# Two residual additions moved to TensorE with an identity and written out by ScalarE, in a convolution-attention and selective-scan kernel

## The chip, the cores and the metric

The kernel runs on one core of one Trainium2 chip. The time is the device time of one execution in microseconds (us). A core has five engines with a queue each: TensorE (PE; its weight loads are shown apart as PEld), VectorE (DVE), ScalarE (ACT), GpSimd (POOL) and SyncE (SP), which here issues nearly all DMA transfers. PSUM is the memory that TensorE writes; POOL's instructions in this kernel never touch it.

## The reference, cut to what is computed

Eight images of 256 channels and 48 x 48 = 2304 positions pass through two residual layers:

```
x = x + attention(groupnorm(x))            # layer 0
x = x + mamba2(mamba1(groupnorm(x)))       # layer 1, two scan blocks

def attention(x):                          # per image, tokens: 2304 x 256
    feat, pos = split(tokens @ W.T + bias)          # 2304 x 256 each
    pos = pos / max(norm(pos), 1e-12)
    sim = pos @ pos.T                               # 2304 x 2304
    topksim, topkid = top_k(sim, 16)
    return softmax(topksim) weighted sum of feat[topkid]

def mamba(x):                              # 2304 positions, 512 inner channels, 16 states
    x = layernorm(x) * w + b
    xi, z = split(x @ in_w.T)
    xc = silu(causal_conv4(xi) + cb)
    dt_r, B, C = split(xc @ xp_w.T);  dt = softplus(dt_r @ dtp_w.T + dtp_b)
    h[t] = h[t-1] * exp(dt[t] * A) + dt[t] * B[t] * xc[t]
    y = sum over states of h * C + D * xc
    return (y * silu(z)) @ out_w.T
```

The two additions that the change concerns are `x + attention(...)` and the last `x + ...` after the second scan block.

## The kernel before

**Outline.** Layer 0 of image 0 runs alone at the start (`layer0(0, ..., True)`, about the first 470 us). After that the scans of image b run together with layer 0 of image b + 1, instruction by instruction, in an order written out by hand. The last image's scans have no layer 0 beside them.

**The scan's units and half-steps.** Positions are cut into 6 chunks of 384. A *unit* is one chunk of one scan block, so that an image has 12 units, numbered 0 to 11 here in their order (c, d) = (0,0), (1,0), (2,0), (0,1), (3,0), (1,1), (4,0), (2,1), (5,0), (3,1), (4,1), (5,1); d is the scan block. A unit has 16 steps of two *half-steps*, 32 half-steps in all, called h0 to h31 below. There are 8 x 12 x 32 = 3072 half-steps. In each one DVE runs one scan instruction (`run_scan`, L843; 770 elements on 128 partitions).

**What surrounds a scan.** ACT writes its decays into one of two PSUM areas with two exponentials (`decay`, L828), one half-step ahead; POOL makes the scan's input for two half-steps at once (`make_bx`, L804), two steps ahead. The product of the states with C is made either by POOL (L871, in `pool_part`, for one or both half-steps of a step at once) or by DVE (L845, right behind the scan). Which, is set by `SHARE`: one letter for each half-step, G for POOL (GpSimd) and V for DVE. It has three patterns, for units 1 to 9 of images 0 to 6 (called stage 0 here), for units 0, 10 and 11 of these (stage 1), and for the last image (stage 2). In a V half-step the scan writes the PSUM area, and ACT takes the last state from there (`carry`, L859); otherwise `carry_pool` (L881) takes it from SBUF. TensorE then sums the states (`sum_states`, L886 and L889) into a PSUM tile `y`, which DVE multiplies into z (`gate`, L895). The tables `between` and `behind` place all other work of a unit on half-steps relative to its first; `between` runs ahead of the scan of its half-step and `behind` after it.

**The first block's way out.** `out_proj` (L907, at 38, so in h6 of the next unit) makes the two outputs `pw` of 128 channels in PSUM, and `leave` (at 39 and 40, h7 and h8 of the next unit) brings each out. For d = 0 ACT copies it to SBUF (L920) and SP stores it. For d = 1 DVE adds it to the residual `res`, loaded in `load_out` (L924), and SP stores it to the output.

**Layer 0 beside the scans.** `layer0` is a generator that is advanced once at the end of each half-step (`ahead.go`). Its attention works on 18 blocks of 128 rows per image. The table `within` gives each piece of a block a part, block t's part p being executed in half-step 38 + 16 t + p of the image: `similar` makes the 5 pieces of a row of similarities (TensorE, tile `psim`), `keep_similar` copies them out (ACT, L408), `top` finds the 16 greatest (DVE, 4 instructions of 2304 elements), `average` scales the weighted sum (ACT, tile `o`) and loads the block of x (tile `xr`), `turn_back` transposes `o` into the PSUM tile `pr` (L482), and `finish` (part 24, so h14 or h30) adds `pr`, the bias and `xr` on DVE (L491), takes the statistics (L495) and has SP store the sum to `x1`. When all blocks are done, `group_stats` spreads over 8 half-steps; `load_v` of the next image's first unit, 42 half-steps ahead of it, calls `ahead.finish`, which runs whatever of the generator is left.

**PSUM slots.** All these PSUM tiles (`pe`, `pw`, `y`, `psim`, `pr`, `pt` and so on) share one tag "mm" of 3 slots when layer 0 runs beside scans (5 when it runs alone). A tile can be written only when an earlier tile's last reader is done.

Of the kernel before, what the change touches and what calls it, by code (L numbers as in the profile page):

```python
# [10 lines left out]
AF = mybir.ActivationFunctionType  # L11
ALU = mybir.AluOpType
# [3 lines left out]
P = 128  # L16
# [9 lines left out]
def tile_conv_preact(  # L26
# [18 lines left out]
    nc = tc.nc  # L45
    B, C, N = x.shape
    DEPTH, DI, NS = A_log.shape
# [3 lines left out]
    CB = C // P  # L51
    DB = DI // P
# [5 lines left out]
    G = 32  # L58
# [4 lines left out]
    PARTS = Q // HQ  # L63
# [4 lines left out]
    BLOCK = 16  # L68
# [1 line left out]
    PHASE = 6  # L70


    SHARE = ("GGVGGGVVGGGGGGVG", "GGGVGVVGVVVGVGVG", "VGVGVGVVGGVVGGVG")
    assert N % T == 0 and N % P == 0 and T % P == 0 and NS % (J * HQ) == 0

    const = ctx.enter_context(tc.tile_pool(name="const", bufs=1))
# [10 lines left out]
    ident = const.tile([P, P], F32, tag="ident", name="ident")  # L87
# [32 lines left out]
    b_feat = const.tile([P, CB], F32, tag="b_feat", name="b_feat")  # L120
# [109 lines left out]
    def layer0(b, left, pool, ps0, alone):  # L230
        def mm0(w, name):
            return ps0.tile([P, 512], F32, tag="mm", name=name, bufs=5 if alone else 3)[:, :w]
# [159 lines left out]
        blocks = [{} for _ in range(NB)]  # L392
# [85 lines left out]
        def turn_back(t):  # L478
            row = blocks[t]
            row["pr"] = mm0(C, f"pr_{b}_{t}")  # L480
            for cb in range(CB):
                nc.tensor.transpose(  # L482
                    row["pr"][:, cb * P : (cb + 1) * P], row["o"][:, cb * P : (cb + 1) * P], ident
                )

        def finish(t):
            row = blocks[t]
            xr = row["xr"]

            for cb in range(CB):  # L490
                nc.vector.scalar_tensor_tensor(  # L491
                    xr[:, cb, :], row["pr"][:, cb * P : (cb + 1) * P], b_feat[:, cb : cb + 1],
                    xr[:, cb, :], ALU.add, ALU.add,
                )
                nc.vector.bn_stats(st1[:, cb, t, :], xr[:, cb, :])  # L495
            nc.sync.dma_start(x1[:, t * P : (t + 1) * P].rearrange("(k p) t -> p k t", p=P), xr)
            row.clear()


        within = [  # L500
            (21, weights, 3), (4, top, 3), (14, turn, 0), (15, weights, 0), (6, others, 3),
            (-5, similar, 4), (-8, keep_similar, 0), (-5, keep_similar, 2), (24, turn_back), (18, weigh, 1),
            (17, weigh, 0), (1, top, 1), (-9, similar, 0), (-8, similar, 1), (-7, similar, 2),
            (22, average), (-6, similar, 3), (-7, keep_similar, 1), (-3, keep_similar, 3), (0, top, 0),
            (-3, keep_similar, 4), (15, turn, 1), (10, others, 4), (5, others, 0), (3, top, 2),
            (6, add_top), (11, invert), (5, others, 2), (17, turn, 2), (20, turn, 3),
            (15, weights, 1), (18, turn, 4), (18, weights, 2), (21, weigh, 3), (7, others, 1),
            (19, weigh, 2), (20, weights, 4), (21, weigh, 4), (24, finish),
        ]
        begin = min(part for part, *_ in within)  # L510
        parts = {}
# [13 lines left out]
    with tc.tile_pool(name="first", bufs=1) as pool0, tc.tile_pool(  # L525
        name="first_ps", bufs=1, space=PSUM
    ) as ps0:
        for _ in layer0(0, lefts[0], pool0, ps0, True):
            pass
# [28 lines left out]
    def mm(w, name):  # L558
        return ps.tile([P, 512], F32, tag="mm", name=name, bufs=3)[:, :w]
# [232 lines left out]
    def on_pool(unit, i, p):  # L792

        stage = 2 if unit["b"] + 1 == B else 0 if TOPK[0] <= unit["at"] < TOPK[1] else 1
        return SHARE[stage][(i * PARTS + p) % BLOCK] == "G"

    def make_bx(n):

# [34 lines left out]
    def run_scan(m):  # L833
        n, p = divmod(m, PARTS)
        if not 0 <= n < NSTEP:
            return
        unit, i, k = at(n)
        qs = slice(p * HQ, (p + 1) * HQ)
        bx = unit["bx"][i][:, qs]
        g = bx.rearrange("p q t -> p (q t)")  # L840
        da = decays(m)
        h = g if on_pool(unit, i, p) else da
        nc.vector.tensor_tensor_scan(h, da, g, 0.0, ALU.mult, ALU.add)  # L843
        if h is da:
            nc.vector.tensor_tensor(  # L845
                bx[:, :, 0:T], da.rearrange("p (q t) -> p q t", q=HQ)[:, :, 1:],
                unit["BC"][1][:, qs], ALU.mult,
            )

    def carry(m):  # L850

        n, p = divmod(m, PARTS)
        if not 0 <= n < NSTEP:
            return
        unit, i, k = at(n)
        if not on_pool(unit, i, p):
            h = decays(m).rearrange("p (q t) -> p q t", q=HQ)
            if unit["c"] + 1 < NCH:
                nc.scalar.copy(h_st[:, unit["d"], i, p * HQ : (p + 1) * HQ], h[:, :, T])  # L859

    def pool_part(n):

        if not 0 <= n < NSTEP:
            return
        unit, i, k = at(n)
        lo = [p for p in range(PARTS) if on_pool(unit, i, p)]
        if not lo:
            return
        qs = slice(lo[0] * HQ, (lo[-1] + 1) * HQ)
        g = unit["bx"][i][:, qs]  # L870
        nc.gpsimd.tensor_tensor(g[:, :, 0:T], g[:, :, 1:], unit["BC"][1][:, qs], ALU.mult)  # L871
# [31 lines left out]

    def out_proj(unit, cb):
        pw = unit["pw"][cb] = mm(T, f"pw_{unit['u']}_{cb}")
        for k in range(DB):
            nc.tensor.matmul(  # L907
                pw, unit["ow"][:, k, cb * P : (cb + 1) * P], unit["z"][k],
                start=(k == 0), stop=(k == DB - 1),
            )  # L910

    def leave(unit, cb):

        b, c, rows = unit["b"], unit["c"], slice(cb * P, (cb + 1) * P)
        if unit["d"] + 1 < DEPTH:
            v1 = unit["left"].setdefault("v1", {})
            if c not in v1:
                v1[c] = hbm.tile([C, T], F32, tag="v1", name=f"v1_{b}_{c}", bufs=2 * BEHIND)
            vo = keep.tile([P, T], F32, tag="dtx", name=f"vo_{unit['u']}_{cb}")
            nc.scalar.copy(vo, unit["pw"][cb])  # L920
            nc.sync.dma_start(v1[c][rows, :], vo)
        else:
            res = unit["res"]
            nc.vector.tensor_add(res[:, cb, :], res[:, cb, :], unit["pw"][cb])  # L924
            nc.sync.dma_start(out[b, rows, c * T : (c + 1) * T], res[:, cb, :])


# [1 line left out]
    between = [  # L929
        (-35, center), (7, in_proj, 5), (24, sum_states, 2), (-33, variance), (-21, in_proj, 0),  # L930
        (-15, taps, 1), (38, out_proj, 0), (-15, taps, 2), (-14, taps, 3), (-34, square),
        (39, leave, 0), (23, load_rep, "dt", 14), (5, load_rep, "dt", 5), (-4, load_bc, 1), (38, out_proj, 1),
        (17, load_d, 2), (-17, tap, 1), (18, load_rep, "dtx", 13), (-8, times_x, 1), (19, gate, 1),
        (-22, normal), (1, load_rep, "dt", 3), (0, load_rep, "dtx", 4), (15, load_rep, "dt", 10), (6, load_rep, "dtx", 7),
# [12 lines left out]
        (-37, affine), (1, times_x, 2), (7, copy_z, 0), (8, load_rep, "dtx", 8), (-17, tap, 2),  # L947
        (-10, softplus), (-16, in_proj, 3), (3, load_rep, "dt", 4), (-29, load_in, 2), (6, in_proj, 7),
        (35, gate, 3), (-2, load_rep, "dtx", 3), (8, copy_z, 1), (40, leave, 1), (-3, times_x, 3),
        (22, load_rep, "dtx", 15), (-16, load_in, 4), (29, load_d, 3), (-37, mean), (-19, taps, 0),  # L950
        (-19, in_proj, 1), (-10, load_bc, 0), (33, sum_states, 3), (-30, root_end), (-9, times_x, 0),
# [8 lines left out]
    class Ahead:  # L960
# [4 lines left out]
        def turn(self, image):  # L965
            self.image, self.begun, self.started = image + 1, None, False
            self.run = iter(())
            if self.image < B:
                self.run = layer0(self.image, lefts[self.image], keep, ps, False)
# [21 lines left out]
    for m in range(first, PARTS * NSTEP - HOOKS + last + 1):  # L991
        n, p = divmod(m, PARTS)
# [57 lines left out]
```

## Time and profile before

| what | value |
|---|---|
| median of 3 runs | 9905.45 us (9903.67 to 9908.92) |
| the profiled execution: its own time | 9898.83 us |
| its span, first to last instruction | 9897.1 us, mean granted TensorE clock 0.889 |
| first scan / last scan starts at | 517.7 us / 9882.3 us |
| the median unit of stage 0 with d = 1 (5, 7, 9) | about 97 us |
| units 4, 6, 8 of stage 0 | about 99 us |
| units of the last image | about 90 us |
| transfers | 1271 MB, 128 GB/s |

The profile's busy times count no register, branch, semaphore or DMA-issuing instruction. A row "L843 DVE ... bx<-da,bx x2040 | 3521.8, 1746 | 190.5 <-ACT da L828 151.4" says that line 843's instruction on DVE, which writes bx from da and bx, ran 2040 times, 3521.8 us in all and 1746 ns each, and that DVE stood idle for 190.5 us just before such instructions, 151.4 us of it until ACT's line 828 was done. In the waits, "A <- B: us, times, longest" says how long A's engine stood idle until B was done. In the timeline the columns are start, duration, engine, line, operation and how many were merged; the brackets give the idle time just ahead. Consecutive instructions of DVE and ACT overlap in the records by some 0.08 us, so that starts are the better measure of what an instruction costs.

### The profile page before, as it was taken

How to read it: one execution, taken by the hardware profiler on the slowest of the kernel's cores; microseconds unless marked ns; L12 is line 12 of the kernel's file. 1: busy time of each engine (PE TensorE's matmuls, PEld its weight loads, DVE VectorE, ACT ScalarE, POOL GpSimd, SP SyncE). 2: the span in 40 equal slices, each digit the busy share in tenths (PEclk: the TensorE clock that was granted, in tenths of full speed). 3: DMA queues.
4: the chain of work that ended last, by engine and by line, in shares of the span. 5: the costliest groups of instructions: out<-in, count | busy, mean ns of one | idle time of the engine just before them, and what ended most of it. 6: DMA issues, size and time to landing. Idle time of an engine off the chain costs nothing. (4 is left out here: it accounts for less than half of the span.)

```text
span 9897.1 us, 133780 instructions
## 1 busy us (share of the span) xinstructions
PE 8000.3 (81%) x36736; PEld 4388.5 (44%) x36736; DVE 8956.8 (90%) x7993; ACT 7322.2 (74%) x15966; POOL 8943.3 (90%) x3927
## 2 busy tenths in 40 slices
PE   8878887788878888788877888778887788866665
PEld 6644544444534454445444445344544444522222
DVE  4589998999989999899998999899998999988998
ACT  4477777778777877777877787777787778766766
POOL 0099999999989999899998999999998999999999
PEclk9989998899989998899988999889998899977777
DMA  1144445444444444444454444444445444444544
GB/s 32 37 133 126 134 130 152 124 132 129 136 142 131 129 134 137 140 126 133 130 148 128 130 128 134 144 132 125 135 128 152 121 133 127 138 136 129 145 138 122
DMA packets 1243503, 1271.37 MB, mean 128 GB/s; under 512 B 266592, under 2 KB 1215840, under 8 KB 1242752
## 3 DMA queue, kind: packets, MB, share of 16 engines
q1 hardware_dynamic: 1230496, 1262.45, 44.7%
q8 instruction: 293, 4.80, 0.2%
q14 instruction: 458, 3.75, 0.1%
q10 hardware_dynamic: 12256, 0.36, 0.1%
HBM read 1048.94 MB, written 212.86 MB: 127 GB/s over the span
## 5 line engine op out<-in xcount | busy, mean ns | idle before, releaser
L804 POOL TENSOR_TENSOR bx<-BC,dtxr 128x1536 f32<-128x1536 f32 x1536 | 5298.4, 3453 | 115.6 <-PE y L889 59.8
L828 ACT ACTIVATE da<-dtr,A_sb 128x385 f32<-128x385 f32 x6144 | 3591.0, 585 | 871.6 <-DVE bx L843 558.0
L843 DVE TENSOR_TENSOR_SCAN bx<-da,bx 128x770 f32<-128x770 f32 x2040 | 3521.8, 1746 | 190.5 <-ACT da L828 151.4
L871 POOL TENSOR_TENSOR bx<-bx,BC 128x1536 f32<-128x1536 f32 (+1 forms) x1320 | 3303.6, 2503 | 217.5 <-DVE bx L843 205.4
L843 DVE TENSOR_TENSOR_SCAN da<-da,bx 128x770 f32<-128x770 f32 x1032 | 1808.8, 1753 | 193.4 <-ACT da L828 149.0
L602 PE MATMUL pe<-vn,inw 128*128 128x384 f32 (+1 forms) x3072 | 1258.9, 543 | 394.1 <-DVE xr L924 87.0
L399 PE MATMUL psim<-pos 128*128 128x512 f32 (+1 forms) x2880 | 1370.8, 608 | 183.5 <-ACT sim L408 74.7
L465 PE MATMUL po<-feat,aT 128*128 128x256 f32 x5184 | 1364.0, 412 | 13.8 <-ACT aT L454 7.6
L889 PE MATMUL y<-bx,sel 128*32 128x384 f32 x12288 | 1221.2, 533 | 44.2 <-POOL bx L871 37.9
L465 PEld LDWEIGHTS po<-feat,aT 128*128 128x128 f32 x5184 | 1029.8, 205 | 361.9 <-issue 113.9
L845 DVE TENSOR_TENSOR bx<-da,BC 128x768 f32<-128x768 f32 x1032 | 988.8, 958 | 35.5
L602 PEld LDWEIGHTS pe<-vn,inw 128*128 128x128 f32 x3072 | 590.1, 206 | 902.6 <-issue 191.2
L399 PEld LDWEIGHTS psim<-pos 128*128 128x128 f32 x2880 | 552.8, 206 | 818.8 <-issue 470.8
L889 PEld LDWEIGHTS y<-bx,sel 128*32 128x32 f32 x12288 | 394.1, 118 | 856.6 <-issue 725.0
L702 DVE SCALAR_TENSOR_TENSOR xc<-pe,cw,xc 128x384 f32<-128x384 f32 x1152 | 695.7, 611 | 42.8 <-ACT xc L694 15.7
L732 PE MATMUL pd<-dbl,dtp_sb 16*128 16x384 f32 x768 | 424.3, 668 | 342.0 <-ACT dt L741 209.0
L859 ACT COPY h_st<-da 128x2 f32<-128x2 f32 x832 | 131.7, 158 | 686.4 <-DVE bx L845 680.0
L454 ACT ACTIVATE aT<-pt 128x512 f32<-128x512 f32 (+1 forms) x720 | 388.1, 548 | 245.9 <-PE pt L446 239.8
L445 PE MATMUL pt<-ident,sim 128*128 128x128 f32 x2592 | 539.6, 291 | 33.7 <-DVE v L666 17.6
L907 PE MATMUL pw<-z,ow 128*128 128x384 f32 x1536 | 531.5, 499 | 15.0 <-DVE v L666 7.0
L437 ACT ACTIVATE rest<-left,three 128x512 bf16<-128x512 f32 (+1 forms) x720 | 467.0, 670 | 59.7 <-DVE left L422 59.7
L446 PE MATMUL pt<-minus,rest 128*128 128x128 bf16 x2592 | 491.6, 225 | 3.2 <-ACT rest L437 3.2
(146 smaller groups left out, 9766.8 us busy)
## 6 DMA issues: line engine op xcount, KB each, us to landing
dtxr<-dtx_d SPq DMA_DIRECT2D x6144, 48.0 KB, 1.8
dtr<-dt_d SPq DMA_DIRECT2D x6144, 48.0 KB, 1.8
BC<-bc_d SPq DMA_DIRECT2D x768, 192.0 KB, 3.7
inw<-in_in_wT_dram SPq DMA_DIRECT2D x768, 128.0 KB, 2.2
dtx_d<-dtx SPq DMA_DIRECT2D x384, 192.0 KB, 2.0
dt_d<-dt SPq DMA_DIRECT2D x384, 192.0 KB, 2.2
ow<-in_out_wT_dram SPq DMA_DIRECT2D x96, 512.0 KB, 4.0
dmat<-diag SPq DMA_DIRECT2D x384, 64.0 KB, 2.3
```

The lines of the kernel that those rows point to most:

```text
L399: nc.tensor.matmul(pm, pos[:, k, t * P : (t + 1) * P], pos[:, k, c0 : c0 + w], start=(k == 0), stop=(k == CB - 1),)
L445: nc.tensor.transpose(pt[:, q], row["sim"][:, r], ident)
L465: nc.tensor.matmul(row["po"], aT[:, m % PT, :], feat[:, m, :], start=(m == 0), stop=(m == NB - 1))
L602: nc.tensor.matmul(pe, w[:, k], unit["vn"][:, k, lo:], start=(k == 0), stop=(k == CB - 1))
L702: nc.vector.scalar_tensor_tensor(unit["xc"][e], unit["pe"][e][:, k : k + T], cw[:, unit["d"], e, k : k + 1], unit["xc"][e], ALU.mult, ALU.add,
L804: nc.gpsimd.tensor_tensor(bx[:, :, 1:], unit["BC"][0], unit["dtxr"][i].unsqueeze(1).to_broadcast([P, Q, T]), ALU.mult,)
L828: nc.scalar.activation(da[:, s * (1 + T) : (s + 1) * (1 + T)], unit["dtr"][i], AF.Exp, scale=A_sb[:, unit["d"], i, p * HQ + s : p * HQ + s ...
L843: nc.vector.tensor_tensor_scan(h, da, g, 0.0, ALU.mult, ALU.add)
L845: nc.vector.tensor_tensor(bx[:, :, 0:T], da.rearrange("p (q t) -> p q t", q=HQ)[:, :, 1:], unit["BC"][1][:, qs], ALU.mult,)
L871: nc.gpsimd.tensor_tensor(g[:, :, 0:T], g[:, :, 1:], unit["BC"][1][:, qs], ALU.mult)
L889: nc.tensor.matmul(y[j * G : (j + 1) * G, :], sel, unit["bx"][k * J + j][:, q, 0:T], start=False, stop=True, skip_group_check=True,)
L907: nc.tensor.matmul(pw, unit["ow"][:, k, cb * P : (cb + 1) * P], unit["z"][k], start=(k == 0), stop=(k == DB - 1),)
```

## The change

`finish` is split. In `turn_back` TensorE now also adds the block of x to `pr`, by a matmul with the identity, for each of the two channel blocks. `finish`, moved from part 24 to 25, lets ACT write `pr` plus bias to SBUF. The new `measure` at part 26 takes the statistics on DVE and has SP store the block. For the second scan block TensorE adds `res` to `pw` by one more matmul with the identity, and ACT copies the sum out in place of DVE's addition. `SHARE` gives one half-step in 32 more to DVE in stage 0 (h27) and two more in stage 2 (h12 and h28).

```diff
-    SHARE = ("GGVGGGVVGGGGGGVG", "GGGVGVVGVVVGVGVG", "VGVGVGVVGGVVGGVG")
+    SHARE = ("GGVGGGVVGGGGGGVGGGVGGGVVGGGVGGVG", "GGGVGVVGVVVGVGVG", "VGVGVGVVGGVVVGVG")
 # turn_back
                 nc.tensor.transpose(
                     row["pr"][:, cb * P : (cb + 1) * P], row["o"][:, cb * P : (cb + 1) * P], ident
                 )
+                nc.tensor.matmul(
+                    row["pr"][:, cb * P : (cb + 1) * P], ident, row["xr"][:, cb, :],
+                    start=False, stop=True, skip_group_check=True,
+                )
 # finish
             for cb in range(CB):
-                nc.vector.scalar_tensor_tensor(
-                    xr[:, cb, :], row["pr"][:, cb * P : (cb + 1) * P], b_feat[:, cb : cb + 1],
-                    xr[:, cb, :], ALU.add, ALU.add,
-                )
+                nc.scalar.activation(
+                    xr[:, cb, :], row["pr"][:, cb * P : (cb + 1) * P], AF.Identity,
+                    bias=b_feat[:, cb : cb + 1],
+                )
+
+        def measure(t):
+            row = blocks[t]
+            xr = row["xr"]
+            for cb in range(CB):
                 nc.vector.bn_stats(st1[:, cb, t, :], xr[:, cb, :])
             nc.sync.dma_start(x1[:, t * P : (t + 1) * P].rearrange("(k p) t -> p k t", p=P), xr)
 # within
-            (19, weigh, 2), (20, weights, 4), (21, weigh, 4), (24, finish),
+            (19, weigh, 2), (20, weights, 4), (21, weigh, 4), (25, finish), (26, measure),
 # on_pool
-        return SHARE[stage][(i * PARTS + p) % BLOCK] == "G"
+        share = SHARE[stage]
+        return share[(i * PARTS + p) % len(share)] == "G"
 # out_proj
+        alone = unit["d"] + 1 < DEPTH
         for k in range(DB):
             nc.tensor.matmul(
                 pw, unit["ow"][:, k, cb * P : (cb + 1) * P], unit["z"][k],
-                start=(k == 0), stop=(k == DB - 1),
+                start=(k == 0), stop=(k == DB - 1 and alone),
             )
+        if not alone:
+            nc.tensor.matmul(pw, ident, unit["res"][:, cb, :], start=False, stop=True)
 # leave, second scan block
-            nc.vector.tensor_add(res[:, cb, :], res[:, cb, :], unit["pw"][cb])
+            nc.scalar.copy(res[:, cb, :], unit["pw"][cb])
```

## The prediction

> **What bounds the kernel now.** I read the page first, then the busy time unit by unit, then the waits, then the order of time around the two additions.
>
> ```profile
> PE 8000.3 (81%) x36736; PEld 4388.5 (44%) x36736; DVE 8956.8 (90%) x7993; ACT 7322.2 (74%) x15966; POOL 8943.3 (90%) x3927
> ```
>
> DVE and POOL are level, so the page cannot say which one sets the pace. The busy time per unit (units 4 to 7 of image 4; columns: stretch, length, then PE, PEld, DVE, ACT, POOL busy):
>
> ```profile
> 5663.10:5762.30 99.20, 86.89 (x411) 48.91 (x410) 95.29 (x87) 78.21 (x174) 96.36 (x35) 0.93 0.46 131
> 5762.30:5860.80 98.50, 86.93 (x411) 48.69 (x410) 94.46 (x85) 78.00 (x174) 96.36 (x35) 0.93 0.46 130
> 5860.80:5960.00 99.20, 86.91 (x411) 48.98 (x410) 95.30 (x87) 78.20 (x174) 96.36 (x35) 0.93 0.47 133
> 5960.00:6056.70 96.70, 85.76 (x411) 48.19 (x410) 94.35 (x85) 77.56 (x173) 96.33 (x35) 0.94 0.46 130
> ```
>
> POOL has 96.3 us of work in every unit, yet units last 96.7 to 99.2. The waits of units 4 to 9 say who waits for whom:
>
> ```profile
> DVE z L895 <- PE y L889: 9.0, 6, 2.4
> DVE bx L843 <- ACT da L828: 7.0, 11, 1.1
> POOL bx L871 <- DVE bx L843: 8.6, 7, 1.7
> ```
>
> DVE waits for PE and ACT and never for POOL; POOL waits for DVE. So the path is DVE with ACT and PE in its gaps, and POOL follows with some 1 us per unit to spare. In the last image it is the same with more room (its units 2 to 10):
>
> ```profile
> DVE da L843 <- ACT da L828: 31.7, 14, 3.2
> DVE bx L843 <- ACT da L828: 28.5, 15, 3.1
> DVE da L843 <- POOL bx L804: 1.1, 2, 0.6
> ```
>
> There a unit lasts about 90 us, DVE works 80.5 of it and POOL 84.1. The exception is c = 0: in unit 3 POOL clears the first column of the scan's input behind its other work, and DVE waits 5.4 us for that (L816). Layer 0 of image 0 alone is TensorE's: 59.34 us busy of 60 between 300 and 360.
>
> [...] behind an ACT instruction that waited 1.64 us (L694 below) everything on ACT stood. [...] The trace has 468 ns for 256 elements out of PSUM (L472)[...].
>
> **Part 1: `leave` of d = 1.** Removed: L924 on DVE, 96 x 537 ns, 0.46 from start to start. It does more harm than that. In unit 6 the third `pe` needs the slot of `pw`, DVE frees it late behind its top-16 work, and everything behind slides:
>
> ```profile
> 5886.65 2.27 PE L602 MATMUL pe<-vn,inw 128*128 128x384 f32 x4 [1.82 <-DVE xr L924]
> ...
> 5897.32 0.56 DVE L895 TENSOR_TENSOR z<-y,z 128x384 f32<-128x384 f32 x1 [2.44 <-PE y L889]
> ```
>
> In unit 7, where ACT empties `pw` (L920, 468 ns), neither wait is there. The two kinds differ by 1.8 us (units 4, 6, 8 against 5, 7, 9, all images), so units 4, 6, 8 should become like 5, 7, 9. Added on ACT: a copy of 468 ns per tile, beside 2.9 us in which ACT waits for DVE at h7; with that cover gone, 0.9 us a unit. Added on PE: one fp32 matmul of 384 columns per tile, two instructions 0.32 us apart, 1.3 us of PE for a unit; unit 7 has about 1.0 us to spare before z is held, so I count 0.1 against. 21 units x -1.7 = **-36 us**. In units 10, 11 and 0, DVE waits at h10 for PE anyway; -0.9 there is lost, and in unit 10, where PE runs without a gap from `pw` to `y`, the 1.3 us lies on the path: 14 units x 0.7 = +10.
>
> **Part 2: `finish`.** Removed on DVE: L491, 288 x 339 ns. With L495 (292 ns) a block costs DVE 1.17 us; the two statistics alone cost 0.5, so 0.68 goes. Added: two ACT instructions, 0.6 us a block, and four short matmuls, 0.45 us. ACT has the room on average (78 of 97 us), but not at that place. Around h14 of unit 6:
>
> ```profile
> 5906.77 0.44 PE L482 MATMUL pr<-ident,o 128*128 128x128 f32 x2 [0.46 <-ACT sim L408]
> 5908.23 1.98 PE L399 MATMUL psim<-pos 128*128 128x512 f32 x4 [1.02 <-DVE xr L491]
> 5910.89 1.98 PE L399 MATMUL psim<-pos 128*128 128x512 f32 x4 [0.68 <-ACT sim L408]
> ```
>
> ```profile
> 5908.79 1.23 ACT L694 ACTIVATE xc<-pe,cbias,cw 128x384 f32<-128x384 f32 x2
> 5910.25 0.58 ACT L408 COPY sim<-psim 128x512 f32<-128x512 f32 x1 [0.24 <-PE psim L399]
> ...
> 5915.31 0.67 ACT L694 ACTIVATE xc<-pe,cbias,cw 128x384 f32<-128x384 f32 x1 [1.64 <-PE pe L602]
> ```
>
> Two slots hold `pe` here, and the one left goes psim, pr, psim, psim. The next psim starts when `finish` has read `pr`, at 5908.2. On ACT, one half-step on, `finish` stands behind two exponentials and two taps (L694), and ends at about 5910.4. Then psim 2.0, its copy 0.65, psim 2.0, pe 1.5: the last tap starts at about 5916.5 instead of 5915.3, while DVE, 0.68 lighter, wants it sooner. The copy (L408) and the decays behind it wait on ACT meanwhile. The silu and decay burst that DVE waits for at h20 (0.5 us today) starts no earlier. For h14: DVE gains nothing, 0 to +0.6. For h30: `pr` has its own slot, but the copy behind `finish` is 0.3 late, two psim and `y` follow, and the gate at h3 has no room: 0 to +0.3. If the slots left room, it would be -0.68. I take +0.1 x 126 blocks = **+13 us**, with ends of -86 and +57. The identity matmul also waits for `xr`: PE reaches `pr` in half of the blocks within 3 us of the issue of that load, which takes 2.3 to land. PE waits about 1 us there, covered by a gap of 1.5 us ahead of L649; if that is gone, +1 us x 63. SP's store moves two half-steps on and then waits for ACT, no more for DVE (622 us in SP's waits, L496): the transfers behind it can only be earlier, and DVE and ACT hardly wait for them (45.7 us in all): 0. `group_stats` comes two half-steps later, and `ahead.finish` now flushes its last three pieces at once, PE to ACT to POOL in one half-step: 0 to 4 us x 7, I take +5.
>
> **Part 3: `SHARE`.** A V adds L845, 958 ns, 0.9 from start to start (a bare G half-step lasts 1.7 us, a bare V one 2.6), and a 0.16 us copy on ACT. At h27, h12 and h28 DVE has no idle time, so it is paid in full: stage 0, 63 units x 0.9 = **+57**; last image, 24 x 0.9 = **+22**. POOL gets a half product for a whole (1685 for 3184 ns): -1.5 us each, 94 + 36 us. As POOL holds nobody up, that is worth nothing, but for unit 3, where POOL comes to its clearing some 3 us earlier: 7 x -3 = -21, and -3 in the last image.
>
> **Part 4: image 0 alone.** PE is full there: 18 blocks x 0.45 = **+8**. DVE and ACT have room: 0.
>
> **The sum.** 8 + 57 - 36 + 13 - 21 + 10 + 5 + 22 - 3 = +55 us on the profiled execution's 9898.8 (span 9897.1 and 1.7 around it), which lies 0.07% under the median of 9905.45. On the median: 9960 us. What 0.2%, about what a measurement tells from no change, means here is 20 us.
>
> **Rivals.** (A) *The freed DVE time comes through.* ACT has about 2.3 us idle between h27 and h33, PE about 10 a unit; if the slot chain gives room, part 2 is -86 instead of +13: 55 - 99 = -44, 9861 us. For it: unit 1 has no block to finish at h14, and h14 is 1.1 us shorter there with nothing paid back by h20. Against it: unit 1 has no `pr` in the slot either. It decides once more than about half of the 0.68 us comes through. (B) *POOL is the real bound.* It is busy 99% of the shorter units. Then 94 + 36 us less POOL work counts: about -130, 9775 us. Against it: DVE never waits for POOL outside c = 0. (C) *Balance*: half of (A), within 20 us of no change. (D) *PE and ACT tighter than I think*: part 2 at +57, the xr wait uncovered in part, units 0 and 10 at +1.3: +120, 10025 us.
>
> **Numbers.** Slower, as forecast or as (D): 0.52; (C) 0.16; (A) 0.25; (B) 0.07. The range takes in (A) and (D): 9840 to 10030; the forecast's own is 9925 to 10030.
>
> **What would show it.** Right: units 5, 7, 9 about 1 us longer, h27 up by 0.9; units 4, 6, 8 close to them, the wait of `pe` on L924 gone; psim waiting on ACT longer than the 1.0 us it waited on L491; POOL's idle time up by 2 us a unit; the last image up by about 20 us. Wrong: DVE's idle time in units 5, 7, 9 unchanged with DVE's busy time down, or DVE waiting for POOL in the kernel before at places that the records don't show.

## The result and the profile after

The changed kernel takes 10003.24 us (median of 4 runs, 10000.49 to 10011.81), the kernel before 9907.00 us in the same series: a ratio of 1.0099, with a 95% interval of 1.0081 to 1.0116. It is slower by 96 us; 9960 had been forecast, 9840 to 10030 as the range, so the result lies inside it and toward its upper end. The profiled execution has a span of 9998.7 us at a mean granted clock of 0.881.

In the changed kernel `psim` (L399) and the copy of sim (L408) keep their lines. ScalarE's `finish` is L495, the statistics are L504, the identity matmul of `xr` is L485; L828 has become L838 (decay), L843 L853 (scan), L694 L703 (tap), L702 L711 (taps), L889 L899 (y), L895 L905 (gate), L816 L826 (the clearing for c = 0).

The page's busy line:

```profile
PE 8157.6 (82%) x37504; PEld 4525.2 (45%) x37504; DVE 8916.9 (89%) x7696; ACT 7432.4 (74%) x16426; POOL 8823.2 (88%) x3927
```

DVE has 40 us less to do than before, POOL 120 us less; ACT has 110 and PE 157 us more. The two busiest engines are lighter and the kernel is longer, so idle time has been added to the path. Busy time unit by unit (units 4 to 7 of image 4; columns as in the view of before):

```profile
5719.10:5818.50 99.40, 89.45 (x422) 50.76 (x422) 94.47 (x82) 79.94 (x182) 95.05 (x35) 0.91 0.47 132
5818.50:5918.90 100.40, 89.39 (x416) 50.69 (x417) 94.30 (x81) 78.85 (x180) 94.92 (x35) 0.90 0.45 126
5918.90:6018.40 99.50, 88.14 (x426) 50.28 (x425) 94.31 (x82) 80.14 (x183) 95.03 (x35) 0.93 0.47 133
6018.40:6117.40 99.00, 87.16 (x414) 49.63 (x414) 94.23 (x82) 78.50 (x179) 94.89 (x35) 0.92 0.45 127
```

Units 4 and 6 stand where they stood, 5 and 7 are 1.9 and 2.3 us longer, and the difference between the two kinds is gone. (On average over images 0 to 6, units 5, 7 and 9 are 2.8, 2.0 and 1.3 us longer; about 1 had been expected.) POOL now has 4.1 to 5.5 us to spare in each. The waits of units 4 to 9:

```profile
PE psim L399 <- ACT xr L495: 21.3, 11, 3.2
ACT sim L408 <- PE psim L399: 32.7, 15, 3.9
DVE bx L853 <- ACT da L838: 18.0, 21, 1.4
DVE xc L711 <- ACT xc L703: 4.8, 6, 1.4
DVE z L905 <- PE y L899: 3.0, 5, 0.7
```

DVE's wait for `y` has shrunk from 9.0 to 3.0 us (that was the slot which L924 used to hold), its wait for ACT's decays has grown from 7.0 to 18.0, and above them stands a chain that is new in this size: `psim` waits up to 3.2 us for `finish` on ACT, and ACT waits up to 3.9 us for `psim`. In the last image DVE waits for the decays as before:

```profile
DVE da L853 <- ACT da L838: 32.7, 23, 2.3
DVE bx L853 <- ACT da L838: 18.0, 6, 3.1
```

**Where a block loses.** The timeline around h14 to h17 of unit 6 in image 4, the place that the prediction worked through:

```profile
5965.16 1.23 ACT L703 ACTIVATE xc<-pe,cbias,cw 128x384 f32<-128x384 f32 x2
...
5966.28 0.62 ACT L495 ACTIVATE xr<-pr,b_feat 128x128 f32<-128x128 f32 x2
...
5966.95 6.34 PE L399 MATMUL psim<-pos 128*128 128x512 f32 x8 [3.15 <-ACT xr L495]
...
5970.77 0.59 ACT L408 COPY sim<-psim 128x512 f32<-128x512 f32 x1 [3.87 <-PE psim L399]
5971.25 1.21 ACT L838 ACTIVATE da<-dtr,A_sb 128x385 f32<-128x385 f32 x2
...
5972.49 1.76 DVE L853 TENSOR_TENSOR_SCAN bx<-da,bx 128x770 f32<-128x770 f32 x1 [1.44 <-ACT da L838]
...
5974.63 0.67 ACT L703 ACTIVATE xc<-pe,cbias,cw 128x384 f32<-128x384 f32 x1 [0.44 <-PE pe L611]
```

h14 starts at 5961.0 here. `finish` stands behind two taps, and `psim` starts 5.95 us into h14, against 3.6 us before. The four matmuls that its copy needs then take 3.8 us (5966.95 to 5970.7) where they took 1.98. So the copy starts 9.8 us into h14 instead of 5.65, and the decay stands behind it in ACT's queue: DVE waits 1.44 us for it ahead of the scan of h17. The last tap comes 13.6 us in, not 10.7, and DVE's taps wait for that too. Added up over images 0 to 6, DVE waits 49 us for the decays ahead of h17 and 46 us for the last tap behind it; in the kernel before these two waits are 0.2 us together.

### The profile page after: what moved, and what is told of

It reads as the page before. It is cut to its first block, busy times and chain, and to the rows that moved or that the text cites. A ratio compares the mean times of both kernels' runs of the same rounds, so it can differ in the third digit from the quotient of the medians.

```text
span 9998.7 us, 135654 instructions
## 1 busy us (share of the span) xinstructions
PE 8157.6 (82%) x37504; PEld 4525.2 (45%) x37504; DVE 8916.9 (89%) x7696; ACT 7432.4 (74%) x16426; POOL 8823.2 (88%) x3927
## 3 DMA queue, kind: packets, MB, share of 16 engines
q14 instruction: 461, 3.78, 0.1%
## 5 line engine op out<-in xcount | busy, mean ns | idle before, releaser
L838 ACT ACTIVATE da<-dtr,A_sb 128x385 f32<-128x385 f32 x6144 | 3592.0, 585 | 714.2 <-DVE bx L853 365.0
L853 DVE TENSOR_TENSOR_SCAN bx<-da,bx 128x770 f32<-128x770 f32 x1953 | 3382.7, 1749 | 262.9 <-ACT da L838 228.3
L881 POOL TENSOR_TENSOR bx<-bx,BC 128x1536 f32<-128x1536 f32 (+1 forms) x1320 | 3177.8, 2407 | 293.8 <-DVE bx L853 233.8
L853 DVE TENSOR_TENSOR_SCAN da<-da,bx 128x770 f32<-128x770 f32 x1119 | 1962.1, 1753 | 238.4 <-ACT da L838 191.1
L399 PE MATMUL psim<-pos 128*128 128x512 f32 (+1 forms) x2880 | 1433.5, 635 | 248.8 <-ACT xr L495 203.0
L899 PE MATMUL y<-bx,sel 128*32 128x384 f32 x12288 | 1194.6, 527 | 25.8 <-DVE bx L855 19.4
L855 DVE TENSOR_TENSOR bx<-da,BC 128x768 f32<-128x768 f32 x1119 | 1072.2, 958 | 38.5
L399 PEld LDWEIGHTS psim<-pos 128*128 128x128 f32 x2880 | 589.2, 216 | 886.7 <-issue 533.0
L711 DVE SCALAR_TENSOR_TENSOR xc<-pe,cw,xc 128x384 f32<-128x384 f32 x1152 | 697.2, 612 | 87.5 <-ACT xc L703 60.5
L899 PEld LDWEIGHTS y<-bx,sel 128*32 128x32 f32 x12288 | 386.9, 117 | 821.7 <-issue 742.9
L408 ACT COPY sim<-psim 128x512 f32<-128x512 f32 (+1 forms) x720 | 379.9, 536 | 342.4 <-PE psim L399 342.1
L454 ACT ACTIVATE aT<-pt 128x512 f32<-128x512 f32 (+1 forms) x720 | 388.2, 549 | 253.8 <-PE pt L446 249.0
```

What stands on the lines that cost most here:

```text
L399: nc.tensor.matmul(pm, pos[:, k, t * P : (t + 1) * P], pos[:, k, c0 : c0 + w], start=(k == 0), stop=(k == CB - 1),)
L711: nc.vector.scalar_tensor_tensor(unit["xc"][e], unit["pe"][e][:, k : k + T], cw[:, unit["d"], e, k : k + 1], unit["xc"][e], ALU.mult, ALU.add,
L838: nc.scalar.activation(da[:, s * (1 + T) : (s + 1) * (1 + T)], unit["dtr"][i], AF.Exp, scale=A_sb[:, unit["d"], i, p * HQ + s : p * HQ + s ...
L855: nc.vector.tensor_tensor(bx[:, :, 0:T], da.rearrange("p (q t) -> p q t", q=HQ)[:, :, 1:], unit["BC"][1][:, qs], ALU.mult,)
L899: nc.tensor.matmul(y[j * G : (j + 1) * G, :], sel, unit["bx"][k * J + j][:, q, 0:T], start=False, stop=True, skip_group_check=True,)
```

## The experiments

The next table adds up where each kernel's half-steps differ from those of the kernel before, from the starts of DVE's scans in the profiled executions (us; images 0 to 6, all units; the stretch h21 to h24 changes by at most 1.6 and is left out). The last image is counted from its first scan to its last. The last column is the difference of the medians, each against the kernel before in its own series of runs.

| kernel | ahead of the first scan | h4-12 (leave) | h13-20 (finish at h14) | h25-28 (V at h27) | h29-h3 (finish at h30) | last image | medians |
|---|---|---|---|---|---|---|---|
| changed | +11.1 | -18.7 | +77.1 | +63.9 | -48.1 | +17.5 | +96 |
| both additions, old SHARE | +10.3 | -27.0 | +92.1 | +0.3 | -31.6 | +1.6 | +44 |
| new SHARE alone | +1.6 | +12.1 | +7.7 | +64.2 | -22.8 | +16.7 | +73 |
| leave alone | -0.8 | -25.6 | +9.2 | -0.2 | +8.3 | -1.9 | -15 |
| finish alone | +10.8 | +4.4 | +95.3 | -0.2 | -28.8 | -1.9 | +76 |
| early load (below) | -6.1 | -24.3 | -5.3 | 0.0 | -37.8 | -4.2 | -81 |
| clearings on ScalarE (below) | -5.7 | -39.5 | -26.7 | 0.0 | -68.2 | +4.2 | -149 |

A stretch that an edit doesn't touch moves by 9 to 12 us (h13-20 with leave alone, h4-12 with the new SHARE alone), so smaller entries say nothing.

**1. SHARE put back.**

```diff
-    SHARE = ("GGVGGGVVGGGGGGVGGGVGGGVVGGGVGGVG", "GGGVGVVGVVVGVGVG", "VGVGVGVVGGVVVGVG")
+    SHARE = ("GGVGGGVVGGGGGGVG", "GGGVGVVGVVVGVGVG", "VGVGVGVVGGVVGGVG")
```

> The change with the old SHARE put back: leave and finish stay on TensorE and ScalarE, VectorE and GpSimd divide the scan products as in the kernel before. Theory (the path is VectorE's; every half-step turned from G to V is paid at about 0.9 us, and GpSimd's relief is worth only some 10 us): 75 us below the changed kernel, so about 9930 us, still some 25 us above the kernel before. Rival, GpSimd sets the pace: its 130 us of work come back and nothing else, so 10040 us or more. Rival, the losses come from ScalarE and TensorE alone (SHARE costs nothing because VectorE had the freed time to spare): about 10000 us, as the changed kernel.

Measured: 9949.47 us, ratio to the kernel before 1.0050 (1.0033 to 1.0066). SHARE made 52 of the 96 us (96 less 44). GpSimd is not the bound: with its work back the kernel is faster, not slower. The two additions cost 44 us, more than the 25 expected.

**2. The new SHARE alone**, in the kernel before.

> The kernel before with the new SHARE alone; both additions stay on VectorE. Theory (VectorE's path): 63 + 24 more products on VectorE at 0.9 us, less some 10 us for GpSimd's earlier clearing in unit 3: about +70 us, 9975 us. Rival, GpSimd sets the pace: about -100 us, 9800 us. Rival, the new SHARE costs something only because ScalarE and TensorE were made late by the other two parts: within 20 us of the kernel before.

Measured: 9978.26 us, ratio 1.0072 (1.0057 to 1.0087). Its page:

```profile
PE 8007.3 (80%) x36736; PEld 4381.2 (44%) x36736; DVE 9042.8 (91%) x8080; ACT 7357.1 (74%) x16042; POOL 8823.7 (88%) x3927
```

POOL works 120 us less than before, DVE 86 more, and the kernel is 73 us longer: DVE's time is paid, POOL's relief is not repaid. h27 is 1.0 us longer in every one of the 63 units. Units 2 and 3 get 1.0 and 2.0 us shorter in h29 to h3, because POOL comes to the clearing (L816) sooner: -21 us.

**3. Leave of d = 1 alone** (identity matmul into `pw`, ACT's copy).

```diff
-            nc.vector.tensor_add(res[:, cb, :], res[:, cb, :], unit["pw"][cb])
+            nc.scalar.copy(res[:, cb, :], unit["pw"][cb])
```

> The kernel before with the second scan block's addition alone on TensorE and ScalarE (leave of d = 1). Theory: units 4, 6 and 8 are 1.8 us shorter in images 0 to 6, the others as before, units 0, 10 and 11 a little longer: -25 us, 9882 us. Rival (TensorE is the bound here: the identity matmul is added to it and gives back what VectorE gains): within 20 us of the kernel before or above. Rival (all 96 freed additions come through at 0.46 us): -44 us or more on top of the 36, 9825 us.

Measured: 9890.39 us, ratio 0.9987 (0.9980 to 0.9994). Units 4, 6 and 8 are 1.8, 1.9 and 1.8 us shorter in h4 to h12. Units 10 and 11 lose 1.3 and 1.9, unit 0 gains 1.5. In unit 10 of image 4 (h8 to h10) PE runs from `pw` to `y` without a gap, and DVE waits for the decays first and for `y` after that:

```profile
DVE z L895 <- PE y L889: 4.0, 1, 4.0
DVE da L843 <- ACT da L828: 2.5, 1, 2.5
```

The wait for `y` is 4.0 us in the kernel before as well; the wait for the decays was 0.3 there. ACT's copy of `pt` (L454) waits 1.92 us for PE, and the decays stand behind it.

**4. Finish alone** (identity matmul of `xr`, `finish` on ACT at part 25, `measure` at 26).

> The kernel before with the attention's addition alone on TensorE and ScalarE (identity matmul of xr, finish on ScalarE, statistics one half-step later). Theory (the slot of pr is freed late behind ScalarE's queue, so copy of sim, pe and tap are late and VectorE waits at h17, which eats the 0.68 us taken off VectorE): +11 us before the first scan and +0.3 to +0.7 us a block after it, about +45 us, 9952 us. Rival (the freed VectorE time comes through): 126 blocks x -0.68 us + 11 us = -75 us, 9830 us. Rival (loss and gain cancel): +11 us, the first image's part alone, 9917 us.

Measured: 9981.47 us, ratio 1.0077 (1.0062 to 1.0092). It is the dearest part, and it loses at h14 (+95 us, 1.5 a block) while it gains at h30 (-29 us). Taken alone the three parts come to 134 us, together they cost 96: with finish in, leave is worth -32, and the new SHARE costs 52 rather than 73. A part of that can be placed: with finish alone, DVE's wait for POOL's clearing at h31 of unit 2 grows from 5.5 to 13.6 us (seven images), and in the changed kernel, where POOL comes to the clearing sooner, it is zero. What was not tried is `finish` on ACT at its old part 24: no run separates the change of engine from the move by one half-step.

**5. `pr` in a place of its own.** Both additions moved, old SHARE; `pr` takes the half of the block's `po` bank that lies unused.

```diff
-                row["po"] = ps0.tile([P, 512], F32, tag="po", name=f"po_{b}_{t}", bufs=more)[:, :C]
+                row["bank"] = ps0.tile([P, 512], F32, tag="po", name=f"po_{b}_{t}", bufs=more)
+                row["po"] = row["bank"][:, :C]
-            row["pr"] = mm0(C, f"pr_{b}_{t}")
+            row["pr"] = row["bank"][:, C : 2 * C]
```

> Old SHARE, both additions on TensorE and ScalarE as in the change, but pr lies in the unused second half of the block's own po bank instead of in one of the three mm slots. Theory (finish frees the mm slot late, and psim, copy of sim, pe and tap slide behind it): VectorE's wait at h16 and h17, 1.0 to 2.3 us a block, goes and the 0.7 us of each finish come through; 63 blocks x about -2 us = -125 us against the same kernel with pr in a slot (9949 us), about 9825 us, and psim waits for xr no more. Rival (it is ScalarE's own 0.6 us ahead of the taps, not the slot): psim starts sooner but the taps of channel block 3 are late as before, VectorE still waits at h17, 9935 to 9955 us. Rival (TensorE's added matmuls are the cost): as before, about 9950 us.

Measured: 9872.35 us, ratio 0.9974 (0.9966 to 0.9982), so 73 us better than experiment 1, each against its own series, not 125. (The profiled execution took 9900.2 us, the longest of the 13 runs, so its waits are read here and not its length.) In experiment 1 `psim` waited for `finish`, in this line of its waits:

```profile
PE psim L399 <- ACT xr L495: 195.3, 99, 3.4
```

That wait is gone. At h16 and h17 the loss is gone: 9.3 to 9.6 us for the two in units 2 to 9, against 10.4 to 12.0 in experiment 1 and 8.84 in the kernel before, which has its statistics (0.46 us) elsewhere. That it was the slot, and not ACT's added 0.6 us, is shown: ACT does the same work in both. DVE's waits for the decays ahead of h17 and for the last tap behind it, 55 and 50 us in experiment 1 (images 0 to 6), are 0 and 9 here. What was won came back elsewhere as waits of another kind:

```profile
PE po L486 <- DMA xr<-in_x_dram: 150.0, 58, 5.3
```

TensorE now comes to the identity matmul before `xr` has landed (76.2 us over the whole kernel in experiment 1), and `psim` stands behind it.

**6. The same place in the kernel before**, both additions on VectorE.

> The kernel before with only pr moved into the second half of its po bank; both additions stay on VectorE, no work is added or taken away. If VectorE's path already paid for that slot in the kernel before (psim waits 1.0 us for L491): -20 to -35 us, about 9875 us. If the slot only costs when ScalarE frees it late, as in the changed kernel: within 20 us of 9905 us.

Measured: 9885.61 us, ratio 0.9986 (0.9979 to 0.9993). It is 16 us below the kernel before in the same series, so the second expectation holds, if only just. h16 and h17 are as long as before (8.84 us): the slot costs nothing at h14 as long as DVE frees it in time. But the 16 us have a place. DVE's waits for `y`, in the kernel before and here:

```profile
DVE z L895 <- PE y L889: 117.7, 69, 4.3
DVE z L896 <- PE y L890: 98.2, 63, 4.0
```

At h3, behind the block that finishes at h30, this wait falls from 19.3 to 4.3 us over images 0 to 6; in every other kernel of this document it lies between 16 and 34 us there. So the slot did cost some 15 us in the kernel before, at the gate at h3 and not at h14.

**7. Two parts given back to VectorE**: image 0, and leave of the units at 9 to 11.

```diff
+        alone = unit["d"] + 1 < DEPTH or unit["at"] >= TOPK[1] - 1
 # leave: tensor_add on VectorE for the same units ...
 # finish, image 0 (and no identity matmul there) ...
+                if alone:
+                    nc.vector.scalar_tensor_tensor(...)
+                    continue
```

> As the run with pr in its own bank, and two more edits: image 0, which is TensorE's alone, keeps its additions on VectorE, and leave of d = 1 stays on VectorE for the units at 9, 10 and 11, whose leave falls in units 10, 11 and 0. Theory: -11 us ahead of the first scan, and 2.2 us less in unit 10 and 2.0 us less in unit 11, 1.4 us more in unit 0, x 7 = -20 us: 30 us below that run, so about 9795 us. Rival (what is saved there is waited for in the next unit): only the 11 us, 9815 us. If the theory of the slot is wrong, 30 us below 9949 us, 9920 us.

Measured: 9858.61 us, ratio 0.9956 (0.9941 to 0.9971): 14 us below experiment 5, and far from the 9795 of the theory, which had taken experiment 5 at 9825. The first scan starts 5 us sooner and units 10 and 11 are 1.8 and 1.4 us shorter; the medians show about half of the 30 us. Its timeline at the end of unit 7 of image 4 shows what still stands in the way:

```profile
6039.21 0.80 PE L487 MATMUL po<-xr,ident 128*128 128x128 f32 x2 [4.99 <-DMA xr<-in_x_dram]
...
6040.44 3.58 PE L399 MATMUL psim<-pos 128*128 128x512 f32 x4
...
6044.05 0.59 ACT L408 COPY sim<-psim 128x512 f32<-128x512 f32 x1 [2.74 <-PE psim L399]
...
6045.78 1.76 DVE L860 TENSOR_TENSOR_SCAN bx<-da,bx 128x770 f32<-128x770 f32 x1 [3.06 <-ACT da L845]
```

It is the chain of above with another head: a late load, slow `psim`, a late copy, decays behind it, DVE idle for 3 us.

**8. The load of `xr` five half-steps earlier**, on top of 7.

```diff
-            (19, weigh, 2), (20, weights, 4), (21, weigh, 4), (25, finish), (26, measure),
+            (19, weigh, 2), (20, weights, 4), (21, weigh, 4), (25, finish), (26, measure), (17, fetch),
```

> As the run with pr in its own bank, image 0 and the last three leaves on VectorE (9859 us), and the load of xr moved from half-step 22 to half-step 17 of each block. Theory (TensorE stands up to 5 us for that load ahead of pr, its psim and the decays behind the copy of sim come late, and VectorE waits 2 to 4 us at h0 to h2 of units 6 and 8 and 2.7 us at h14 of unit 2): 6 to 8 us an image, -45 us, about 9815 us, and TensorE's wait for xr gone. Rival (GpSimd, which has under 0.5 us idle in units 4, 5, 7 and 9 there, is the bound by now): the waits move, at most -15 us, 9845 us.

Measured: 9818.21 us, ratio 0.9919 (0.9904 to 0.9933), 40 us below experiment 7 and 3 us from the theory's number. PE's waits for that load are gone. That the number fits is in part luck: 6 to 8 us an image were expected from units 2, 6 and 8, and of these only unit 8 is shorter, by 4.9 us (units 2 and 6 changed by about 0.2); the first scan starts 5 us sooner, which was not in the theory. The same place as in the timeline of the changed kernel (unit 6, h14 at 5858.9):

```profile
5864.23 0.62 ACT L506 ACTIVATE xr<-po,b_feat 128x128 f32<-128x128 f32 x2
5864.73 0.60 ACT L408 COPY sim<-psim 128x512 f32<-128x512 f32 x1
...
5865.26 3.74 DVE L722 SCALAR_TENSOR_TENSOR xc<-pe,cw,xc 128x384 f32<-128x384 f32 x6
...
5868.91 1.75 DVE L863 TENSOR_TENSOR_SCAN bx<-da,bx 128x770 f32<-128x770 f32 x1
```

The copy follows `finish` at once, its `psim` long done, and the scan of h17 follows DVE's taps without a gap, 10.0 us into h14 (11.5 in the changed kernel, 10.8 in the kernel before).

**9. The early load alone, in the changed kernel.**

> The changed kernel with nothing but the load of xr moved to half-step 17. Theory (there psim waits for finish on ScalarE anyway, and TensorE stands only 28 us in all for that load): -5 to -20 us, about 9990 us. Rival (the load is the cause of the late psim in the changed kernel too, as in the run with pr in its own bank): -45 us or more, 9955 us.

Measured: 10035.89 us, ratio 1.0134 (1.0116 to 1.0151). Neither expectation: it is slower than the changed kernel, by an amount at which the two intervals just meet. PE's wait for the load is gone and nothing is won, as the theory had it; the loss it had not. In the records a matmul of `psim` takes 645 ns on average instead of 635, and in the groups of the last section TensorE's granted clock is 0.57 on average instead of 0.65; why it is lower here stays open.

**10. The new SHARE on top of 8.**

> As the run with pr in its own bank, image 0 and the last three leaves on VectorE and the early load, and the new SHARE of the change on top (63 + 24 products more on VectorE, 130 us less on GpSimd). Theory (VectorE's path): the same kernel with the old SHARE + 60 us, about 9875 us. Rival (with VectorE lighter, GpSimd has become the bound of units 4 to 9, and this is the balance that the new SHARE is for): 20 us or more below the same kernel with the old SHARE, 9795 us. Balance: within 20 us of it.

Measured: 9847.56 us, ratio 0.9945 (0.9930 to 0.9960), 29 us above experiment 8. 17.9 us of it are the last image. In images 0 to 6 the V half-steps are paid at 1.0 us again, 64 us, and in the profiled executions 56 of that come back: units 2 and 3 are 3.2 and 0.5 us shorter all the same, units 5, 6, 7 and 9 stay within 0.3, and only 4 and 8 keep a loss (2.6 and 2.0).

**11. The clearings for c = 0 on ScalarE**, on top of 8. `none` is a small tile cleared once; for every other c ACT writes these columns anyway.

```diff
-            nc.gpsimd.memset(vn[:, :, 0:H], 0.0)
+            nc.scalar.copy(vn[:, :, 0:H], none[:, 0 : CB * H].rearrange("p (k h) -> p k h", k=CB))
-            nc.gpsimd.memset(unit["bx"][i][:, :, 0], 0.0)
+            nc.scalar.copy(unit["bx"][i][:, :, 0], none[:, CB * H :])
```

> As the run with the early load (9818 us), and the first columns of c = 0 (of bx and of vn) written by ScalarE from a cleared tile, as ScalarE already writes them for every other c, no longer by GpSimd behind its own queue. Theory (these clearings are the only place at which VectorE waits for GpSimd: 61 us on bx in all, and 2.9 us an image in unit 2, where pe waits for vn): -60 to -80 us, about 9750 us. Rival (GpSimd, without idle time in units 4 to 9, is the bound; what is won in units 2 and 3 is waited for later): -20 us, about 9800 us.

What it removes, from the waits of experiment 8 over the whole kernel:

```profile
DVE bx L863 <- POOL bx L836: 39.0, 18, 5.3
DVE da L863 <- POOL bx L836: 21.7, 23, 2.0
```

Measured: 9754.85 us, ratio 0.9851 (0.9836 to 0.9866): 63 us below experiment 8, and the fastest kernel of all. Units 2 and 3 are 4.9 and 4.6 us shorter. Units 4 to 7 of image 4 now:

```profile
5574.30:5671.50 97.20, 89.76 (x423) 50.60 (x422) 93.34 (x81) 79.45 (x181) 97.20 (x35) 0.92 0.49 133
5671.50:5767.70 96.20, 85.97 (x420) 49.47 (x419) 93.12 (x79) 78.58 (x179) 96.20 (x35) 0.95 0.50 135
5767.70:5863.40 95.70, 87.25 (x422) 49.59 (x422) 93.27 (x81) 79.59 (x181) 95.70 (x35) 0.95 0.49 136
5863.40:5959.40 96.00, 86.13 (x420) 49.15 (x419) 93.10 (x79) 78.47 (x178) 96.00 (x35) 0.95 0.47 129
```

POOL is busy from the first to the last microsecond of each, so at about 96 us these units have reached the length of POOL's work.

**12. The new SHARE of stage 0 on top of 11.**

> As the run with the clearings on ScalarE, and the new SHARE of the change in stage 0 alone (63 products from GpSimd to VectorE). Theory (part of what the new SHARE gave back came from the clearings in units 2 and 3, 4 to 5 us an image, and that is gone; in units 4 to 9 GpSimd is no longer short, which gave 5 us back for 6 paid): the run with the old SHARE + 20 to + 40 us. Rival (GpSimd's 1.5 us a unit are still the bound of units 4 to 9): the run with the old SHARE - 20 us or lower. Balance: within 20 us of it.

Measured: 9803.47 us, ratio 0.9900 (0.9883 to 0.9916), 49 us above experiment 11. Taking 1.5 us off a POOL without idle time saves less than the 1.0 us that it costs DVE: images 0 to 6 pay 64 us at h27 and get 19 back. That is beyond the upper end of what was expected.

## Why the prediction was right or wrong, step by step

**What bounds the kernel: right.** DVE with ACT and PE in its gaps; POOL's relief worth nothing but at the clearing. Experiments 1 and 2 show both (rival B is out), and 120 us less of POOL's work, set against the 1.0 us at h27, shortened no unit of stage 0 by more than 0.4 us but 2 and 3. It is right for the kernel before; in the kernel of experiment 11 POOL has no idle time left in units 4 to 7 of image 4.

**Part 3, SHARE: right.** +57 was said and +64 measured at h27, 1.0 us each instead of 0.9; -21 in unit 3, and -21 measured, though one third of it lies at the end of unit 2; +19 net in the last image, +16.7 to +17.5 measured.

**Part 1, leave: right, and by its own mechanism, with some luck in the sum.** -36 + 10 = -26; alone it gave -25.6 in h4 to h12. The second term was better in its sum than in its parts: units 10 and 11 lose 1.3 and 1.9, unit 0 gains 1.5, where units 10 and 0 were to lose 0.7 each; the errors cancel. The median moved by 15 only. The wait of `pe` for the slot of `pw` is gone in units 0, 4, 6 and 8 (64 us over images 0 to 6 before); in unit 11 it grew from 4 to 26 us and is now one for ACT's copy, which the working did not have.

**Part 2, finish: the step that failed, as the size of a term.** It was +13, with ends of -86 and +57. Measured alone, h13 to h20 and h29 to h3 add up to +66, past the upper end; in the changed kernel, with the 21 us of the clearing taken off the second stretch, to +50. That is 37 of the some 41 us by which the whole forecast was too low. Two entries of the working are wrong, on opposite sides.

- *h14, "0 to +0.6": measured +1.5 a block.* That `finish` would end about 2.2 us later was right (2.3); the 0.6 us for its two instructions was the author's estimate, and they take 0.62. Wrong was the `psim` of 2.0 us after it: behind waits of 2.96 to 3.24 us on PE its four matmuls took 1.98 to 3.78. And "the copy and the decays behind it wait on ACT meanwhile" was written down and priced at nothing: these decays make up half of the loss (49 us of DVE's wait, ahead of h17), and the last tap, which came 2.9 us late, not 1.2, the other half (46 us). Experiment 5 removes the slot from this chain and the loss with it.
- *h30, "0 to +0.3": measured about -0.5 a block.* DVE's 0.68 us came through here: with finish alone h30 is 73 us shorter in all, of which the statistics take back 28 at h0, and that is 0.70 a block. The gate at h3, which was to take all of it, took about 3 us (DVE's wait for `y` there is 22 us over images 0 to 6 instead of 19). More than half of what was lost again lies at the end of unit 2, where h31 is 8 us longer in all, in DVE's wait for POOL's clearing; part 2 had no entry for that.

**Part 2, the rest.** Image 0 alone, +8: +11. That the wait for the load of `xr` is covered was right for the changed kernel (PE stands for it for 27.7 us in all, and experiment 9 wins nothing by removing it); the "+1 if the cover is gone" was right in kind and too small: in experiment 7 up to 5 us stood open in single units, and experiment 8 won 40 us. The flush of `group_stats`, +5: finish alone shows +9 at h8 and h9 of unit 11, but the new SHARE alone, which leaves the flush as it is, shows +7 there, so whether the flush cost anything stays open.

**The rivals.** The result lies nearer to (D), 10025, than to the forecast: its first element, part 2 at +57, is what happened; of the other two, only unit 10's +1.3 did (with leave alone). (A), 44 us below the kernel before, is what the same change comes to once `pr` leaves the slot and the load is early (52 below in experiment 10, where image 0 and three leaves are back on VectorE): "if the slots left room" was the right condition.

## What to carry to other kernels

When work is moved from a busy engine to one with idle time, look at what the moved instruction releases and at whose queue it now stands in: here 0.62 us on ScalarE held a PSUM slot for 2.3 us more, and a copy ahead of the decays passed it on to VectorE. Give the intermediate a place of its own and issue its load earlier before judging the move: the same two additions went from +44 to -81 us that way, with a little given back to VectorE. And an engine that is busy 90% of the time, as GpSimd is in the kernel before (8943.3 of 9897.1 us), isn't the bound for that: ask who waits for it, and where; GpSimd's one place of weight was worth 63 us, and copies of 0.2 us on ScalarE removed it.

## What the runs showed of the hardware

A wait on TensorE was paid twice here. Within `psim`, where matmuls follow back to back, I took the distance from the first to the fourth start. In the kernel before, after waits of 1.02 to 1.34 us for `finish` (56 groups), a matmul of 512 columns comes every 0.46 us, and no group is above 0.47. In the changed kernel, after waits of 2.96 to 3.24 us (56 groups), every 0.75 us on average: ten groups below 0.5, 25 at 0.9 or more. In experiment 9 the waits are as long (3.14 us on average) and the distance is 0.82, with one group below 0.5. The trace's record of the granted clock goes with it: the 56 groups of the kernel before ran at 1.00 of the clock; in the changed kernel the ten groups below 0.5 us ran at 1.00, the 25 at 0.9 or more at 0.50, and all 56 at 0.65 on average; the 56 of experiment 9 ran at 0.57. The stretches at half clock in the spans of the two kernels (305 before, 348 after) last 3.41 us or whole multiples of it. What starts such a stretch was not shown, and the length of the wait alone does not tell: after waits of 2.96 to 3.24 us some groups ran at 1.00 and some at 0.50, in the changed kernel 28 of the 36 groups after waits of 0.5 to 0.9 us are above 0.5 us, and in experiment 8, after waits of 2.3 us, 28 of 62 are. Here the slow matmuls lie on the path at h14, in every second block.
